# Where an attention step takes in another stream's transposes, and where their copy out of PSUM stands

## The chip, the cores and the metric

The kernel runs on one core of a Trainium2 chip. Its time is the device time of one execution in microseconds (us), the median of several. A core has engines with instruction queues of their own: TensorE (PE in the profile; PEld are its weight loads), VectorE (DVE), ScalarE (ACT), GpSimd (POOL) and SyncE (SP, which here only issues DMAs). TensorE writes to PSUM, from where ScalarE or VectorE have to copy a result before its PSUM buffer can be used again. An engine runs its instructions in the order of its queue, and an instruction that waits for another engine holds up all that are queued behind it.

## The reference

16 graphs of 1024 nodes with 128 features, and a dense 1024 x 1024 weighted adjacency matrix for each:

```python
h = relu(layernorm(x))
# layer 0: attention with 8 heads, masked and weighted by the adjacency
scores = where(adj == 0, -inf, q @ k.T / sqrt(16))        # each head
attn = softmax(scores) * adj
attn = attn / (attn.sum(-1) + 1e-8)
x = x + (attn @ v) @ Wo.T + bo
# layer 1: "dilation" of the adjacency, then three graph convolutions
h = relu(layernorm(x))
for n in range(1024):                                      # each graph, row after row
    num = row.sum();  sf = ceil(num / 2) if num > 10 else 1
    rm = row & (cumsum(row) % sf == 0) & (num > 1)         # edges of row n to remove
    carry[n] &= ~rm;  carry[:, n] &= ~rm                   # in the row and in the column
adj_d = adj * carry
for i in 1, 2, 3:
    h = batchnorm(relu(l2norm((adj_d @ h / deg) @ Wr + h @ Wx + b)))
x = x + concat(h1, h2, h3) @ Wl + bl
```

Attention and dilation both need the adjacency alone of the big inputs, and neither needs the other's result.

## The kernel before

The function `swept` does all of it, in two stages. In the first, which fills about the first 2330 us, two streams of work share the engines: `attention()` and `dilation()`, both generators. `beside_attention` (L951) runs them: after each step of the attention it lets the dilation go on to its next `yield`, for as long as the dilation's spent cost (the first number of each `yield`) is below its share. The second value of a `yield` says when the dilation may go on: 0 at once, 1 after the next attention step, "A" after the next step with even number, "B" after the next with odd number. For TensorE, ScalarE and VectorE the order in which the program issues instructions is the order of the queue (a "manual schedule"). The order on SP and POOL is set by a planner. The second stage, the graph convolutions, follows and isn't touched.

**The attention** goes through 16 graphs x 2 halves of the queries x 8 blocks of 128 keys, and for each through two groups of four heads, g = 0 and g = 1. So there are 512 steps; g = 0 are the even ones ("A") and g = 1 the odd ones ("B"). One step issues, in this order:

- `scores` (L539), on TensorE: 16 small matmuls put the mask into two PSUM tiles `sc` (L554), eight more add the score products (L560). There are two buffers of `sc`, just these two tiles, so the scores of a step can start only as the exponentials of the step before have read them: the first half of the mask matmuls needs the first exponential done, the second half the second.
- for g = 0, a normalization's two ScalarE instructions (L288), if one is due, and the transposes of an adjacency tile (`turn_over`, L505) on TensorE; for g = 1, a TensorE piece of the preparation of the next graph or of the conclusion of the last (`go_on_with(True)`: transposes or products, such as L401, L414, L333, L424).
- `values` (L484) of the step before, on TensorE: L487 and L492, which need that step's VectorE products `w` and exponentials `e`.
- two exponentials `e` (L598) on ScalarE, each over 128 x 1024 of `sc`, and then two products `w` (L603) on VectorE.
- the copies out of PSUM of the pieces above, on ScalarE (`go_on_with("evict")`); for g = 0 `aT` (L508) and `nomask` (L512) with their DMAs on SP, of which six shift the mask by partitions.

**The dilation** goes through eight blocks of 128 rows, for all 16 graphs together. In a block it first finds what each row removes within the block (VectorE mostly), and there it has transposes of its own: `pd` (L772) and `pr` (L878), two batches of eight bf16 transposes each in a block, into the PSUM tile `ps_d` of which there is one. Then it goes graph by graph through the 16 matrices, in a loop of 18 turns `i` (L896 to L949) that is a small pipeline. A turn has two parts. The first is issued after an A step: a scan of matrix i (`pair_sums`, L900, VectorE), and for matrix i - 2 eight transposes of its removal rows `er` (`pe`, L907, TensorE) and their copy `et` (L909, ScalarE, 128 x 1024 bf16). Then it yields "B". The second part is issued after the B step: two activations `wr` of matrix i (L915, ScalarE), the rows `er` of matrix i - 1 (L924 to L930, VectorE), the reading of the next block's adjacency rows as signs for matrix i - 2 (`read`, L699 and L703, ScalarE), the update of the diagonal of `er` with `et` (L937, VectorE), the stores of `er` and `et` to `mr_d` (L938 to L942, SP), `survive` (L716, VectorE), and loads for the next turns.

So in the kernel before, TensorE meets the transposes L907 between the values in an A step and the scores of the B step that follows; ScalarE meets the copy L909 after the A step's `nomask` and before the B step's exponentials.

Of the kernel before, what the change touches and what calls it, by code (L numbers as in the profile page):

```python
# [11 lines left out]
BF = mybir.dt.bfloat16  # L12
# [4 lines left out]
ALU = mybir.AluOpType  # L17
# [4 lines left out]
P = 128  # L22
# [12 lines left out]
def swept(ctx: ExitStack, tc: tile.TileContext, t: dict, out: bass.AP, flag: bass.AP):  # L35
# [8 lines left out]
    nc = tc.nc  # L44
    x, adj, nodemask = t["x"], t["adj"], t["nodemask"]
    B, N, D = x.shape
    H = 8
    HD = D // H
    NB = N // P
# [13 lines left out]
    ident_bf = const.tile([P, P], BF, name="ident_bf")  # L63
# [99 lines left out]
    ps_d = ctx.enter_context(tc.tile_pool(name="ps_d", bufs=1, space=PSUM))  # L163
# [3 lines left out]
    def first_part(p1):  # L167

        pool = p1.enter_context(tc.tile_pool(name="p1", bufs=2))
# [294 lines left out]

        beside = []

        def take_on(steps, at):
            beside.insert(at, [steps, next(steps)])

        def go_on_with(*kinds):  # L470


            for steps in beside[::-1] if kinds == ("first",) else beside:
                if steps[1] in kinds:
                    steps[1] = next(steps[0], None)
                    if steps[1] is None:
                        beside.remove(steps)
                    return

        def attention():  # L480
# [86 lines left out]
            for i, (b, c, m) in enumerate(turns):  # L567
                if m == 0:
                    if c == 0:
                        xt, _, _, v1 = ready[b]  # L570
                    acc = [ps_o.tile([P, HN], F32, name=f"acc_{b}_{c}_{g}", tag=f"acc{g}") for g in range(2)]
                    if c == 0 and b + 1 < B:
                        take_on(prepare(b + 1), len(beside))
                    if c == 1 and b + 1 == B:
                        take_on(begin_sage(), len(beside))
                if c == 1 and m == HB + 1:
                    load_x(b + 2)
                load(i + 3)
                aT = tiles[i][0]
                for g in range(2):  # L580
                    scs = scores(i, g)
                    go_on_with(f"half {c}")
                    if g == 0:
                        go_on_with("first")
                        turning = turn_over(i + 2)
                        next(turning, None)
                    else:
                        go_on_with(True)
                    if late:
                        values(*late)  # L590
                    elif g == 0:
                        go_on_with(True)
                    if (i, g) == (2, 0):
                        node_masks()
                    es, ws = [], []
                    for q in range(2):
                        e = pool.tile([P, 2, HN], F32, name=f"e_{b}_{c}_{m}_{g}_{q}", tag="e", bufs=4)
                        nc.scalar.activation(e, scs[q], AF.Exp, scale=1.0 / math.sqrt(HD))  # L598
                        es.append(e)
                    go_on_with("evict by VectorE")  # L600
                    for q in range(2):
                        w = pool.tile([P, 2, HN], F32, name=f"w_{b}_{c}_{m}_{g}_{q}", tag="w", bufs=4)
                        nc.vector.tensor_tensor(w, es[q], aT.to_broadcast([P, 2, HN]), ALU.mult)  # L603
                        ws.append(w)
                    late = (acc, v1, m, g, es, ws)
                    if m == 0 and g == 0 and i > 0:

                        take_on(conclude(*done), 1 if c == 0 else 0)
                        go_on_with(False)
                    go_on_with("evict")  # L610
                    if g == 0:
                        next(turning, None)
                    go_on_with(False)
                    if i + g + 1 < len(turns):
                        made["next"] = partial(scores, i + g, 1 - g)
                    yield
                tiles.pop(i)
                done = (b, c, acc, xt)
# [21 lines left out]
        def twice(ap):  # L640

            return ap.unsqueeze(2).to_broadcast([P, B, 2])
# [8 lines left out]
        def dilation():  # L651
# [84 lines left out]
            for k in range(NB):  # L736
# [3 lines left out]
                dgs = [rks[i][:, :, 2 + n0 : 2 + n1] for i in range(2)]  # L740
                halves = [slice(0, B // 2), slice(B // 2, B)]

                up = shared.tile([P, B, P], F16, name=f"up_{k}", tag="mr", bufs=4)
# [7 lines left out]
                next(late, None)  # L751
                yield 1.3, 1
                w = shared.tile([P, B, P], F16, name=f"w_{k}", tag="mr", bufs=4)
                pd = None
                for hb in halves:
                    nc.vector.tensor_tensor_scan(
                        w[:, hb, :].rearrange("p b i -> p (b i)"),
# [5 lines left out]
                    yield 2.3, 1  # L763
                for _ in late:
                    pass
                valid = shared.tile([P, B, P], BF, name=f"valid_{k}", tag="mr", bufs=4)
                cs = small.tile([P, 6, B], F32, name=f"cs_{k}", tag="cs", bufs=2)
                total, most, half, onw, last1, prev = (cs[:, i, :] for i in range(6))
                for c, hb in enumerate(halves):
                    pd = ps_d.tile([P, B // 2, P], BF, name=f"pd_{k}_{c}", tag="d")  # L770
                    for b in range(B // 2):
                        nc.tensor.transpose(pd[:, b, :], dgs[c][:, b, :], ident_bf)  # L772
                    if c == 0:
                        nc.vector.tensor_scalar(onw, w[:, :, P - 1], 1024.0, None, ALU.subtract)
                        for dg, of in zip(dgs, halves):
                            nc.vector.tensor_reduce(last1[:, of], dg, AX.X, ALU.add)
                    else:

                        nc.vector.tensor_tensor(total, left, right, ALU.add)
                        nc.vector.tensor_tensor(total, total, last1, ALU.add)  # L780
                        nc.vector.tensor_tensor(most, total, kill[:, :, k], ALU.add)
                        nc.vector.tensor_tensor(onw, onw, right, ALU.add)
                        nc.vector.scalar_tensor_tensor(half, total, -0.5, onw, ALU.mult, ALU.add)
                        nc.vector.tensor_scalar(half, half, 0.25, None, ALU.add)
                        end16 = small.tile([P, B, 2], F16, name=f"end16_{k}", tag="at16", bufs=2)
                        nc.vector.tensor_scalar(end16, twice(onw), 1024.0, None, ALU.add)
                    yield (2.5 if c == 0 else 1.4), 1
                    nc.vector.tensor_tensor(valid[:, hb, :], pd, up[:, hb, :], ALU.mult)
                    yield 0.7, 1 - c

                nc.vector.tensor_tensor(valid, valid, each(beyond), ALU.mult)
# [7 lines left out]
                hit = shared.tile([P, B, P], BF, name=f"hit_{k}", tag="mr", bufs=4)  # L799
# [6 lines left out]
                for r in range(ROUNDS):  # L806
# [3 lines left out]
                    num, y, c, high, lost = (v[:, i, :] for i in range(5))  # L810
# [62 lines left out]
                nc.vector.tensor_tensor(hit, hit, valid, ALU.add)  # L873
                yield 2.5, 1
                for c, hb in enumerate(halves):
                    pd = ps_d.tile([P, B // 2, P], BF, name=f"pr_{k}_{c}", tag="d")
                    for b in range(B // 2):
                        nc.tensor.transpose(pd[:, b, :], hit[:, c * B // 2 + b, :], ident_bf)  # L878
                    yield 0.0, 1
                    nc.vector.tensor_tensor(dgs[c], dgs[c], pd, ALU.subtract)  # L880
                    yield 0.7, (1 if c == 0 else "A")


# [3 lines left out]
                wrs, gms, ers, ets = {}, {}, {}, {}  # L887

                def known(b):

                    if k > 0 and b < B:
                        gms[b] = shared.tile([P, N], BF, name=f"gm_{k}_{b}", tag="gm", bufs=2)
                        nc.sync.dma_start(gms[b][:, :n0], mr_d[b][:, k, :n0])

                known(0)
                for i in range(B + 2):  # L896
                    b = i
# [4 lines left out]
                        )  # L902
                    b = i - 2
                    if 0 <= b:
                        pe = ps_d.tile([P, NB, P], BF, name=f"pe_{k}_{b}", tag="d")
                        for j in range(NB):
                            nc.tensor.transpose(pe[:, j, :], ers[b][:, j * P : (j + 1) * P], ident_bf)  # L907
                        ets[b] = pool.tile([P, NB, P], BF, name=f"et_{k}_{b}", tag="et", bufs=2)
                        nc.scalar.copy(ets[b], pe)  # L909
                    yield (1.3 if i < B else 0.0), "B"  # L910
                    b = i
                    if b < B:
                        wrs[b] = pool.tile([P, N], F16, name=f"wr_{k}_{b}", tag="wr", bufs=2)
# [5 lines left out]
                    b = i - 1  # L919
# [12 lines left out]
                    b = i - 2  # L932
                    if 0 <= b:
                        if more:
                            read(k + 1, b)
                        er, et = ers.pop(b), ets.pop(b)
# [275 lines left out]
    with tc.manual_schedule(  # L1212
# [178 lines left out]
        for b in range(B):  # L1391
            pys = products(b)
            of = [pys[k // HB][:, (k % HB) * P : (k % HB + 1) * P] for k in range(NB)]
# [584 lines left out]
```

## Time and profile before

| | us |
|---|---|
| median of 3 runs | 3399.15 (3396.95 to 3402.11) |
| the profiled execution | 3396.91 |
| its span, from first to last instruction | 3395.1 |
| busy in the span: PE, DVE, ACT | 3310.6, 3025.5, 2305.4 |
| granted TensorE clock, share of full | 0.995 |
| copies `et` (L909), 128 of them | 127.2 busy, the first starts at 190.4, the last at 2285.2 |
| transposes `pe` (L907), 1024 of them | 79.4 busy, 18.2 idle before them |
| exponentials (L598), 1024 of them | 991.9 busy, 333.6 idle before them |

A line of the waits names the engine and the line that waited, then after `<-` the one that released it, and the total in us, how often and the longest. A line of the timeline has the start in us, the duration, the engine and line, the operation, `out<-in`, the shapes of out and in, and how many instructions in a row it merges; `[0.22 <-ACT e L598]` is the idle time of that engine just before, and what ended it. Neighbours on ScalarE overlap by some 0.1 us in these records, so a start can lie before the end of the line above. Matmuls are pipelined, and a busy TensorE isn't one at its peak.

### The profile page before, as it was taken

The page shows a single profiled execution, that of the slowest core. Times are in us where ns is not written, and L with a number is a line of the kernel's source. Part 1 is how long each engine was busy: PE and PEld are TensorE (multiplying, and loading weights), DVE is VectorE, ACT ScalarE, POOL GpSimd, SP SyncE. Part 2 cuts the span into 40 slices and gives each one's busy share as a digit, 9 for nine tenths or more (in the row PEclk, how much of TensorE's full clock was granted, in tenths as well). Part 3 has the DMA queues.
Part 4 walks back from the last instruction along what each step waited for, and adds up shares of the span by engine and source line. Part 5 has one row for each costly group of instructions (what it writes and reads, how often), then busy time and mean ns, then how long its engine had stood idle before and what let it go on. Part 6 is the DMA issues. An engine that isn't in the chain of part 4 may idle for free. (4 is left out here: it accounts for less than half of the span.)

```text
span 3395.1 us, 86338 instructions
## 1 busy us (share of the span) xinstructions
PE 3310.6 (98%) x34855; PEld 1872.4 (55%) x34855; DVE 3025.5 (89%) x5399; ACT 2305.4 (68%) x3909; POOL 164.2 (5%) x253
## 2 busy tenths in 40 slices
PE   8999999999999999999999999999999899999997
PEld 3333333333333333333334334336999899999997
DVE  7898989989989998998998999897888899988887
ACT  7699689779879969968976986884232344423334
POOL 2000000000000000000000000000000000000000
PEclk9999999999999999999999999999999999999999
DMA  7357456547637736845863773677999799989996
GB/s 242 108 168 206 137 149 199 161 129 221 188 122 213 221 122 183 238 144 158 236 190 122 237 240 119 189 228 261 346 341 343 284 353 350 353 323 350 352 351 222
DMA packets 650123, 772.28 MB, mean 227 GB/s; under 512 B 173264, under 2 KB 569168, under 8 KB 637424
## 3 DMA queue, kind: packets, MB, share of 16 engines
q1 hardware_dynamic: 632672, 708.58, 64.4%
q0 software_dynamic: 15456, 57.30, 5.0%
q8 instruction: 275, 4.51, 0.6%
q14 instruction: 136, 1.11, 0.1%
q10 hardware_dynamic: 1584, 0.79, 0.1%
HBM read 508.50 MB, written 157.29 MB: 196 GB/s over the span
## 5 line engine op out<-in xcount | busy, mean ns | idle before, releaser
L603 DVE TENSOR_TENSOR w<-e,aT 128x1024 f32<-128x1024 f32 x1024 | 1205.5, 1219 | 138.4 <-ACT e L598 136.8
L598 ACT ACTIVATE e<-sc 128x1024 f32<-128x1024 f32 x1024 | 991.9, 1022 | 333.6 <-PE sc L560 332.6
L1132 PE MATMUL pg<-y,aT 128*128 128x128 f32 (+1 forms) x6144 | 729.8, 275 | 0.0
L1132 PEld LDWEIGHTS pg<-y,aT 128*128 128x128 f32 x6144 | 707.9, 192 | 0.0
L487 PE MATMUL acc<-w,both 128*32 128x512 f32 x4096 | 586.7, 605 | 3.1 <-DVE w L603 2.6
L560 PE MATMUL sc<-qT,kT 32*128 32x512 f32 x4096 | 584.4, 640 | 0.3 <-ACT qT L315 0.3
L492 PE MATMUL acc<-e,eps 128*32 128x512 f32 x4096 | 573.1, 592 | 0.0
L146 DVE SCALAR_TENSOR_TENSOR aT<-mr,aT 128x1024 f32<-128x1024 bf16 x384 | 458.8, 1217 | 0.0
L492 PEld LDWEIGHTS acc<-e,eps 128*32 128x32 f32 x4096 | 150.6, 110 | 294.6 <-issue 289.6
L1155 ACT ACTIVATE sq<-o 128x512 f32<-128x512 f32 x96 | 60.6, 631 | 328.5 <-DVE o L1150 328.5
L554 PEld LDWEIGHTS <-never 32*32 32x32 bf16 x8192 | 80.9, 88 | 347.9 <-issue 325.6
L554 PE MATMUL sc<-nomask,never 32*32 32x512 bf16 x8192 | 252.3, 385 | 16.8 <-ACT e L598 12.3
L1173 ACT COPY hT<-pt 128x512 f32<-128x512 f32 x96 | 56.3, 586 | 289.3 <-PE pt L1169 280.0
L560 PEld LDWEIGHTS sc<-qT,kT 32*128 32x128 f32 x4096 | 160.1, 183 | 116.9 <-issue 116.1
L505 PEld LDWEIGHTS pa<-ident,a 128*128 128x128 f32 x1024 | 107.7, 141 | 181.4 <-issue 129.7
L487 PEld LDWEIGHTS acc<-w,both 128*32 128x32 f32 x4096 | 92.8, 108 | 156.2 <-issue 65.4
L915 ACT ACTIVATE wr<-both,th 128x512 f16<-128x512 f16 x256 | 172.1, 730 | 7.1 <-DVE both L900 6.9
L505 PE MATMUL pa<-ident,a 128*128 128x128 f32 x1024 | 168.3, 287 | 6.4 <-DMA a<-in_adj 5.7
L512 ACT ACTIVATE nomask<-aT 128x512 bf16<-128x512 f32 x256 | 161.4, 630 | 8.1
L1150 DVE SCALAR_TENSOR_TENSOR o<-pg,rdeg,mine 128x128 f32<-128x128 f32 x384 | 108.1, 344 | 55.9 <-PE pg L1132 52.6
L508 ACT COPY aT<-pa 128x512 f32<-128x512 f32 x256 | 152.7, 597 | 5.3 <-PE pa L505 4.3
L900 DVE TENSOR_TENSOR_SCAN both<-rk 128x513 f16<-128x513 bf16 x128 | 155.9, 1218 | 0.0
(228 smaller groups left out, 3894.9 us busy)
## 6 DMA issues: line engine op xcount, KB each, us to landing
aT<-aT_d SPq DMA_DIRECT2D x94, 2048.0 KB, 9.9
mr<-mr_d SPq DMA_DIRECT2D x188, 512.0 KB, 6.0
aT_d<-aT SPq DMA_DIRECT2D x256, 256.0 KB, 4.0
a<-in_adj SPq DMA_DIRECT2D x253, 256.0 KB, 3.7
ad<-in_adj SPq DMA_DIRECT2D x112, 512.0 KB, 4.2
nomask<-nomask SPq DMA_DIRECT2D x512, 96.0 KB, 2.7
nomask<-nomask SPq DMA_DIRECT2D x512, 64.0 KB, 2.7
nomask<-nomask SPq DMA_DIRECT2D x512, 32.0 KB, 2.7
```

The costliest lines, as they stand in the source:

```text
L146: nc.vector.scalar_tensor_tensor(part, mrs[h][:, j : j + 2, :].rearrange("p j n -> p (j n)"), 0.0, part, ALU.is_equal, ALU.mult)
L487: nc.tensor.matmul(acc[g][32 * j : 32 * j + 32, :], v1[:, m, (2 * j + g) * HW : (2 * j + g) * HW + 32], ws[j // 2][:, j % 2, :], start=(m ...
L492: nc.tensor.matmul(acc[g][32 * j : 32 * j + 32, :], eps8, es[j // 2][:, j % 2, :], start=False, stop=(m == NB - 1),)
L505: nc.tensor.transpose(pa[:, k * P : (k + 1) * P], a[:, k, :], ident)
L512: nc.scalar.activation(nomask[:, 0, :], aT[:, 0, :], AF.Relu, bias=1.0, scale=-1e38, accum_out=zeros[:, i : i + 1])
L554: nc.tensor.matmul(scs[j // 2][to : to + 32, j % 2, :], never[rows, rows], nomask[rows, j, :], start=True, stop=False, tile_position=(32 * ...
L560: nc.tensor.matmul(scs[j // 2][:, j % 2, :], kT[rows, mm], qTs[c][rows, g, :], start=False, stop=True, tile_position=(32 * j, 0),)
L598: nc.scalar.activation(e, scs[q], AF.Exp, scale=1.0 / math.sqrt(HD))
L603: nc.vector.tensor_tensor(w, es[q], aT.to_broadcast([P, 2, HN]), ALU.mult)
L900: nc.vector.tensor_tensor_scan(pair_sums[b % 2], row[:, 0::2], row[:, 1::2], 0.0, ALU.add, ALU.add)
L915: nc.scalar.activation(wrs[b][:, t * HN : (t + 1) * HN], pair_sums[b % 2][:, t : t + HN], AF.Abs, bias=at[:, b : b + 1], scale=2.0,)
L1132: nc.tensor.matmul(pg[:, i // 2, at : at + width], aT[:, j, i * P : (i + 1) * P], y[:, j, :width], start=(j == 0), stop=(j == NB - 1),)
```

## The change

Two lists of work are added beside the attention: `ahead_of_values` and `behind_exponentials`. The dilation no longer issues its transposes itself but puts them on the first list, and the copy `et` on the second. The attention's next step issues the first list just ahead of `values`, after the scores and the step's own transposes, and the second behind its exponentials, products and other copies. Where the dilation goes on before that, it issues what is left itself. For matrix i - 2 this means: the transposes L907 move on TensorE from ahead of the scores of the B step to behind them, ahead of the values; the copy moves on ScalarE from ahead of the B step's exponentials to behind them, ahead of the second part's `wr`. The transposes `pd` and `pr` move in the same way by part of a step; VectorE still reads them from PSUM itself.

```diff
+        ahead_of_values, behind_exponentials = [], []
+
+        def run(work):
+            while work:
+                work.pop(0)()
...
+                    run(ahead_of_values)
                     if late:
                         values(*late)
...
                     go_on_with("evict")
                     if g == 0:
                         next(turning, None)
+                    run(behind_exponentials)
                     go_on_with(False)
...
+                pds = []
+
+                def across(name, c):
+                    pd = ps_d.tile([P, B // 2, P], BF, name=f"{name}_{k}_{c}", tag="d")
+                    for b in range(B // 2):
+                        of = dgs[c][:, b, :] if name == "pd" else hit[:, c * B // 2 + b, :]
+                        nc.tensor.transpose(pd[:, b, :], of, ident_bf)
+                    pds.append(pd)
...
-                    pd = ps_d.tile([P, B // 2, P], BF, name=f"pd_{k}_{c}", tag="d")
-                    for b in range(B // 2):
-                        nc.tensor.transpose(pd[:, b, :], dgs[c][:, b, :], ident_bf)
+                    ahead_of_values.append(partial(across, "pd", c))
...
-                    nc.vector.tensor_tensor(valid[:, hb, :], pd, up[:, hb, :], ALU.mult)
+                    run(ahead_of_values)
+                    nc.vector.tensor_tensor(valid[:, hb, :], pds.pop(), up[:, hb, :], ALU.mult)
...
-                    pd = ps_d.tile([P, B // 2, P], BF, name=f"pr_{k}_{c}", tag="d")
-                    for b in range(B // 2):
-                        nc.tensor.transpose(pd[:, b, :], hit[:, c * B // 2 + b, :], ident_bf)
+                    ahead_of_values.append(partial(across, "pr", c))
                     yield 0.0, 1
-                    nc.vector.tensor_tensor(dgs[c], dgs[c], pd, ALU.subtract)
+                    run(ahead_of_values)
+                    nc.vector.tensor_tensor(dgs[c], dgs[c], pds.pop(), ALU.subtract)
...
+                def transposed(b):
+                    pes[b] = ps_d.tile([P, NB, P], BF, name=f"pe_{k}_{b}", tag="d")
+                    for j in range(NB):
+                        nc.tensor.transpose(pes[b][:, j, :], ers[b][:, j * P : (j + 1) * P], ident_bf)
+
+                def emptied(b):
+                    ets[b] = pool.tile([P, NB, P], BF, name=f"et_{k}_{b}", tag="et", bufs=2)
+                    nc.scalar.copy(ets[b], pes.pop(b))
...
-                        pe = ps_d.tile([P, NB, P], BF, name=f"pe_{k}_{b}", tag="d")
-                        for j in range(NB):
-                            nc.tensor.transpose(pe[:, j, :], ers[b][:, j * P : (j + 1) * P], ident_bf)
-                        ets[b] = pool.tile([P, NB, P], BF, name=f"et_{k}_{b}", tag="et", bufs=2)
-                        nc.scalar.copy(ets[b], pe)
+                        ahead_of_values.append(partial(transposed, b))
+                        behind_exponentials.append(partial(emptied, b))
                     yield (1.3 if i < B else 0.0), "B"
+                    run(ahead_of_values)
+                    run(behind_exponentials)
```

More of the change, by code (lines that the diff above doesn't have):

```diff
@@ L753, in dilation @@
                 w = shared.tile([P, B, P], F16, name=f"w_{k}", tag="mr", bufs=4)
-                pd = None
                 for hb in halves:
@@ L893, in known @@
                         nc.sync.dma_start(gms[b][:, :n0], mr_d[b][:, k, :n0])
+                pes = {}
+                def transposed(b):
[5 more added lines that the diff above has]
+                    nc.scalar.copy(ets[b], pes.pop(b))
                 known(0)
```

## The prediction

> **What bounds the kernel now.** I read the page's busy shares first, then the chain of waits, then the busy time by stretch of the span, and last the timeline of one stretch, engine by engine.
>
> ```profile
> PE 3310.6 (98%) x34855; PEld 1872.4 (55%) x34855; DVE 3025.5 (89%) x5399; ACT 2305.4 (68%) x3909; POOL 164.2 (5%) x253
> ```
>
> Over the whole span TensorE looks like the only bound. The waits seem to say the same, and to promise a gain:
>
> ```profile
> ACT e L598 <- PE sc L560: 332.6, 284, 4.0
> ...
> PE pe L907 <- DVE er L930: 18.0, 35, 1.2
> PE sc L554 <- ACT e L598: 12.3, 33, 0.5
> ```
>
> The moved transposes (L907) wait 18.0 us in all for their rows on VectorE, the scores (L554) 12.3 us for exponentials; ScalarE idles 332.6 us for scores. But these are sums over stages. The copies of `et` (L909) show where the moved work runs: eight blocks of some 138 us, 16 copies each, with some 140 us between them without any. The table by stretch has those two kinds in turn (columns: stretch, length, then busy us of PE, PEld, DVE, ACT, POOL with their counts, clock, DMA share, GB/s):
>
> ```profile
> 190.00:328.00 138.00, 135.10 (x1481) 49.86 (x1478) 123.85 (x204) 136.81 (x241) 4.78 (x5) 1.00 0.68 196
> 328.00:465.00 137.00, 136.50 (x1620) 50.44 (x1612) 122.19 (x213) 99.71 (x152) 7.01 (x8) 1.00 0.43 132
> ...
> 1866.00:2011.00 145.00, 139.49 (x1484) 52.24 (x1481) 141.00 (x221) 136.78 (x212) 4.97 (x6) 1.00 0.80 241
> ...
> 2152.00:2286.00 134.00, 131.09 (x1465) 47.56 (x1464) 127.50 (x178) 118.73 (x173) 8.28 (x13) 1.00 0.74 222
> ```
>
> Where the copies run, ScalarE is busy 136.81 of 138 us: it is the bound there, and its idle time lies in the stretches between (99.71 of 137), which have TensorE as the bound and no copies. In the later blocks VectorE joins (141.00 of 145); in the last, ScalarE has slack (118.73 of 134). So the question is what the change does to ScalarE's 9 us per matrix in the blocks. One such period, ScalarE alone:
>
> ```profile
> 1103.62 1.93 ACT L598 ACTIVATE e<-sc 128x1024 f32<-128x1024 f32 x2
> 1105.43 0.60 ACT L508 COPY aT<-pa 128x512 f32<-128x512 f32 x1
> 1106.06 0.63 ACT L512 ACTIVATE nomask<-aT 128x512 bf16<-128x512 f32 x1
> ...
> 1106.69 0.99 ACT L909 COPY et<-pe 128x1024 bf16<-128x1024 bf16 x1
> 1107.59 1.94 ACT L598 ACTIVATE e<-sc 128x1024 f32<-128x1024 f32 x2
> 1109.40 1.34 ACT L915 ACTIVATE wr<-both,th 128x512 f16<-128x512 f16 x2
> ...
> 1111.86 0.88 ACT L288 ACTIVATE xt<-xt,rs_b 128x128 f32<-128x128 f32 x2
> 1112.63 1.92 ACT L598 ACTIVATE e<-sc 128x1024 f32<-128x1024 f32 x2
> ```
>
> No gap anywhere: exponentials of the first head group (g = 0, end 1105.55), aT, nomask, et, exponentials of g = 1 (end 1109.53), then wr, the signs, a normalization, and the next g = 0 (end 1114.55). The period is 9.00 us. TensorE answers like this:
>
> ```profile
> 1105.61 0.41 PE L554 MATMUL sc<-nomask,never 32*32 32x512 bf16 x8 [0.22 <-ACT e L598]
> 1105.94 1.14 PE L560 MATMUL sc<-qT,kT 32*128 32x512 f32 x8
> ```
>
> The second half of the next scores can start only when the last exponential has left its PSUM buffer: 0.06 us after 1105.55. Score products follow at 1105.94, and elsewhere exponentials that find ScalarE idle start 1.17 or 1.18 us after that (1182.66 to 1183.83, 1196.99 to 1198.16). So from the end of one pair of exponentials to the start of the next no less than 0.06 + 0.33 + 1.17 = 1.56 us can pass. The trace has a gap without a copy in it that shows this floor:
>
> ```profile
> 2141.07 1.94 ACT L598 ACTIVATE e<-sc 128x1024 f32<-128x1024 f32 x2
> ...
> 2143.51 0.63 ACT L512 ACTIVATE nomask<-aT 128x512 bf16<-128x512 f32 x1
> ...
> 2144.57 1.94 ACT L598 ACTIVATE e<-sc 128x1024 f32<-128x1024 f32 x2 [0.33 <-PE sc L560]
> ```
>
> End 2143.01, next start 2144.57: 1.56 us, only aT and nomask in it, ScalarE idle at its end. Of all 511 gaps between pairs none is shorter.
>
> **The change, part by part.** No instruction is added or removed. TensorE's L907, pd and pr transposes move, ScalarE's 128 copies move, VectorE's and POOL's order stays; on SP some loads and stores change places with neighbours.
>
> *The copy.* It now stands behind the exponentials of g = 1, not ahead of them. Ahead of them it took 1107.59 - 1106.69 = 0.90 us of the gap g = 0 to g = 1, which lasted 1107.59 - 1105.55 = 2.04 us. Without it ScalarE has aT and nomask to do, done 1106.69 - 1105.55 = 1.14 us after the exponentials; but the scores arrive at 1.56. The gap shrinks by 2.04 - 1.56 = 0.48 us and not by 0.90; ScalarE stands idle 0.42 us. In the gap g = 1 to g = 0, 1112.63 - 1109.53 = 3.10 us and full, the copy adds 0.90. Net 0.90 - 0.48 = +0.42 us a matrix. The copy was the work that hid the turnaround of the scores; the other gap, already twice the floor, needs no cover.
>
> TensorE doesn't stop this. From scores g = 1 (1105.61) its work is 1.40 for the scores, 0.59 for one 4-tile transpose, 0.55 for L907 and 1.85 for the values: next scores at 4.4 us, exponentials possible 1.5 later, at some 6.0. ScalarE comes to them only at 1.56 + 1.94 + 4.00 = 7.5. TensorE just waits longer.
>
> How many pay? By the gaps of ScalarE's timeline, of 80 matrices in blocks 0 to 4, 47 have both gaps full (mean 2.03 first gap): 47 x 0.42 = 19.7 us. In 14 the first gap already has idle time (mean 2.37) and the second is full: without the 0.55 to 0.62 of L907 ahead of the scores it falls to between 1.56 and 1.82, net +0.1 to +0.35, taken as 0.2: 2.8. Ten have two oT copies in the first gap (aT, nomask and these last 2.1, above the floor): nothing. In nine the second gap has some 0.4 us to spare already: nothing. Blocks 5 and 6: ten full (4.2) and five mixed (1.0). Block 7: three, 0.6. Sum 28.3.
>
> *The transposes of L907.* They no longer hold up the scores for a late row. Of their 18.0 us of waiting some 12.4 lies in blocks 5 to 7 (4.5, 5.5 and 2.4 by the timeline). In block 7 TensorE is the bound and 2.4 comes back. In blocks 5 and 6 VectorE is 97% busy, and its order is unchanged; its idle time, 4.6 + 4.0, caps the gain. From 0 to -8.6, I take -2, near the low end, as ScalarE there is as full. In blocks 0 to 4 the wait is behind ScalarE and worth nothing.
>
> Here the Trainium skill speaks the other way. Perfetto Trace Analysis, section Optimization Strategy, says: find the gaps on the engine you are optimizing, see what each waits for, and make that come sooner. Read on the page's 98% TensorE, that rule gives all of 18.0 + 12.3 = 30.3 us: 3369. The same section warns that the most contended engine can change between regimes; the table by stretch shows it does, and then the rule is to be applied to ScalarE, whose gaps the change opens. I go by the table: +24.
>
> *pd and pr.* 32 batches of eight, 0.55 us each, in stretches where TensorE is the bound: same work, one place later. Cover: pd was ready at 1182.36 and used at 1190.30 (L788); one step later it is ready near 1185. pr was made at 155.9 and used at 161.3; it keeps over 2 us. Value 0; if the cover went, at most 32 x 0.6 = 19 us.
>
> *What queues behind the copy.* The wr pair (0.90 later against the exponentials, 0.42 against the period), the signs, the normalization, exponentials: that is the sum above. The VectorE row update L937 uses `et` at 1113.1; the copy now ends about 4.3 after 1105.55, at 1109.9: 3 us of cover. SP's two stores of `et` went out at 1111.12, behind the mask moves that hold SP until 1111.02; 1109.9 is still ahead. If that cover went, SP's loads of `ad` and `gm` behind them would be late, by less than a copy (0.9) a matrix. The other SP swaps are by a few places among issues of 0.3 to 0.6 us, with rows read two periods (18 us) after their load: 0.
>
> *Sum.* 28.3 - 2.4 - 2 = +23.9. The profiled execution took 3396.91 us (span 3395.1), so 3420.8; it lies 2.2 under the median of 3399.15, to which the same +24 gives **3423**. With the bounds: 19.7 alone less 11 gives +9; 28.3 with five more for copies that wait on a long TensorE piece, +33.
>
> **The rivals.** *TensorE's waits are what counts (faster).* L907's 18.0 us comes back and no floor is paid: 3399 - 18 = 3381, with the scores' 12.3 too, 3369. For it: 98% on the page. Against: ScalarE full in the blocks. It decides if the second gap has more than 0.42 us to spare on average; that is so in block 7 only (1.0).
> *Nothing moves (3399).* ScalarE idles over a quarter of the stretches between the blocks, and losses of 0.42 could be taken up. Against: 1.2 us idle in the 138 of block 0.
> *VectorE is starved as well (slower still).* wr was ready at 1110.74 with VectorE coming to it at 1111.03. After the change wr is 0.42 later, 0.13 too late here, and 0.3 to 0.8 too late where VectorE has no normalization beside it. ScalarE's lengthening hides that, unless VectorE is the bound (blocks 3 to 6, 64 matrices): 64 x 0.4 = 26 on top, 3449.
>
> **How the numbers follow.** Copy's cover lost, +9 to +33: 0.63 (3408 to 3432, likeliest 3423). Faster: 0.13. No change: 0.12. VectorE too: 0.12. A measurement tells 0.2% (7 us) from no change; of the main case 0.02 falls inside. Slower 0.73, same 0.14, faster 0.13. The range leaves out most of the faster case and the far end of the starved one: 3390 to 3446.
>
> **What would show it.** Right: in the blocks the gap g = 0 to g = 1 near 1.56 with ScalarE idle 0.4 before exponentials, the other gap near 4.0, the period 9.0 going to 9.4, blocks 0 to 4 each some 4 to 5 us longer, the stretches between unchanged, L907's waits gone, TensorE's waits for exponentials up by tens of us. Wrong: first gaps filled by something that I don't see, periods of 9.0, or blocks shorter than before.

## The result, and the profile after

| us | before | after |
|---|---|---|
| median | 3397.51 (6 runs) | 3422.14 (6 runs, 3418.55 to 3426.26) |
| the profiled execution | 3396.91 | 3420.13 |
| its span | 3395.1 | 3418.3 |
| ratio of the times, 95% interval | | 1.0070 (1.0057 to 1.0083) |

The kernel became 24.6 us slower, 23.2 by the spans of the two profiled executions. The forecast was 3423. Line numbers of the changed kernel are 6 to 24 higher than before: exponentials L605, products `w` L610, mask matmuls L560, score products L566, transposes `pe` L914, copy `et` L918, signs L707 and L711, `survive` L724.

The busy line of the kernel after:

```profile
PE 3302.0 (97%) x34855; PEld 1878.7 (55%) x34855; DVE 3027.9 (89%) x5399; ACT 2309.1 (68%) x3909; POOL 163.9 (5%) x253
```

Counts are the same to the instruction and busy times within 9 us. No engine has more to do; the 23 us are waiting. The chain of waits says who waits:

```profile
ACT e L605 <- PE sc L566: 359.0, 346, 4.7
PE sc L560 <- ACT e L605: 61.7, 135, 0.8
...
DVE rk L724 <- DMA gl<-mr_d: 9.1, 4, 4.4
```

No line names the transposes `pe` any more: the 18.0 us that L907 waited for its rows are gone. In their place TensorE's wait for exponentials rose from 12.3 to 61.7 us, and ScalarE's wait for scores from 332.6 to 359.0. The two wait for each other more often. The third line is new in its size: VectorE waited 2.3 us for `gl` before.

Busy time by stretch of after (stretch, length, then PE, PEld, DVE, ACT, POOL with counts, clock, DMA share, GB/s), the stretches that answer to the four of before:

```profile
191.00:334.00 143.00, 134.09 (x1464) 50.06 (x1456) 123.73 (x205) 137.96 (x240) 4.77 (x5) 1.00 0.66 195
334.00:471.00 137.00, 136.50 (x1628) 51.80 (x1628) 121.89 (x211) 99.23 (x153) 6.81 (x7) 1.00 0.41 126
...
1891.00:2037.00 146.00, 141.83 (x1484) 52.54 (x1482) 142.25 (x224) 137.21 (x213) 4.96 (x6) 1.00 0.80 237
...
2182.00:2314.00 132.00, 130.99 (x1462) 49.88 (x1454) 126.86 (x177) 118.22 (x172) 8.25 (x13) 1.00 0.75 229
```

Block 0 now lasts 143 us where it lasted 138, and ScalarE has worked about as long in it: 1.2 us of idle time have become 5. The stretch behind it has kept its 137 us. Block 6 (third line) grew by 1 us, block 7 (last) lost 2. The granted clock is 1.00 in all of them, so it is not the clock.

The matrix that the prediction showed, on ScalarE of the kernel after:

```profile
1116.51 1.92 ACT L605 ACTIVATE e<-sc 128x1024 f32<-128x1024 f32 x2
1118.32 0.59 ACT L514 COPY aT<-pa 128x512 f32<-128x512 f32 x1
1118.94 0.63 ACT L518 ACTIVATE nomask<-aT 128x512 bf16<-128x512 f32 x1
...
1120.00 1.94 ACT L605 ACTIVATE e<-sc 128x1024 f32<-128x1024 f32 x2 [0.34 <-PE sc L566]
1121.82 1.02 ACT L918 COPY et<-pe 128x1024 bf16<-128x1024 bf16 x1
1122.71 1.35 ACT L939 ACTIVATE wr<-both,th 128x512 f16<-128x512 f16 x2
...
1125.18 0.87 ACT L288 ACTIVATE xt<-xt,rs_b 128x128 f32<-128x128 f32 x2
1125.95 1.92 ACT L605 ACTIVATE e<-sc 128x1024 f32<-128x1024 f32 x2
```

From the end of the exponentials of g = 0 (1118.43) to the start of those of g = 1 pass 1.57 us, with 0.34 of idle time that the scores end. The other gap, 1121.94 to 1125.95, is 4.01 and full. The period is 1125.95 - 1116.51 = 9.44 us; it was 9.00. TensorE in the same gap:

```profile
1118.49 0.41 PE L560 MATMUL sc<-nomask,never 32*32 32x512 bf16 x8 [0.51 <-ACT e L605]
1118.83 1.14 PE L566 MATMUL sc<-qT,kT 32*128 32x512 f32 x8
...
1120.39 0.61 PE L914 MATMUL pe<-ident_bf,er 128*128 128x128 bf16 x8
1120.93 1.06 PE L493 MATMUL acc<-w,both 128*32 128x512 f32 x8
```

TensorE stands ready for 0.51 us, gets the PSUM half 0.06 after the exponentials, and takes 0.34 for the mask; 1.17 after its first score product ScalarE goes on. That is the turnaround of 1.56 us, now without anything to hide it.

Over the whole trace: of 112 gaps g = 0 to g = 1 (the 16 with two more copies, of `oT`, left out) none was under 1.6 us before; after, 86 lie at 1.56, and the idle time in sum went from 14.7 to 46.2 us. The blocks of the two traces, each from its first scan to the first scan behind it:

| | blocks 0 to 4 | 5 and 6 | 7 | stretches ahead of 0 to 4 | ahead of 5, 6, 7 | the rest |
|---|---|---|---|---|---|---|
| growth, us | 5.7, 3.9, 5.0, 3.9, 3.7 | 1.4, 0.5 | -2.3 | -1.9, -0.2, -1.3, -0.3, -0.5 | 1.0, 1.7, 4.5 | -1.7 |
| sum | 22.2 | 1.9 | -2.3 | -4.2 | 7.2 | -1.7 |

The runs of the kernel after differ by up to 8 us, so differences of 1 or 2 us in one stretch mean nothing; the 22.2 of blocks 0 to 4 are the result.

The same two traces can be compared matrix by matrix, by the period from the start of a matrix's g = 0 exponentials to the next start of g = 0. In blocks 0 to 4 the 47 matrices that had both gaps full before grew by 0.44 us each, 20.7 in sum. The 14 that had idle time in the first gap alone grew by 4.3, the ten with two more copies of `oT` shrank by 0.9, and the nine with time to spare in the second gap shrank by 1.9. The sum is the 22.2 again.

### The profile page after: what moved, and what is told of

The parts are those of the page before. It is cut to its first block, busy times and chain, and to the rows that moved or that the text cites. A ratio compares the mean times of both kernels' runs of the same rounds, so it can differ in the third digit from the quotient of the medians.

```text
span 3418.3 us, 86347 instructions
## 1 busy us (share of the span) xinstructions
PE 3302.0 (97%) x34855; PEld 1878.7 (55%) x34855; DVE 3027.9 (89%) x5399; ACT 2309.1 (68%) x3909; POOL 163.9 (5%) x253
## 5 line engine op out<-in xcount | busy, mean ns | idle before, releaser
L610 DVE TENSOR_TENSOR w<-e,aT 128x1024 f32<-128x1024 f32 x1024 | 1205.6, 1219 | 155.6 <-ACT e L605 154.0
L605 ACT ACTIVATE e<-sc 128x1024 f32<-128x1024 f32 x1024 | 991.7, 1022 | 359.8 <-PE sc L566 359.0
L566 PE MATMUL sc<-qT,kT 32*128 32x512 f32 x4096 | 583.9, 640 | 0.5 <-ACT qT L315 0.5
L560 PEld LDWEIGHTS <-never 32*32 32x32 bf16 x8192 | 86.2, 87 | 523.9 <-issue 521.5
L560 PE MATMUL sc<-nomask,never 32*32 32x512 bf16 x8192 | 265.3, 384 | 64.3 <-ACT e L605 61.7
L566 PEld LDWEIGHTS sc<-qT,kT 32*128 32x128 f32 x4096 | 159.9, 182 | 116.9 <-issue 116.1
```

The costliest lines, as they stand in the source:

```text
L560: nc.tensor.matmul(scs[j // 2][to : to + 32, j % 2, :], never[rows, rows], nomask[rows, j, :], start=True, stop=False, tile_position=(32 * ...
L566: nc.tensor.matmul(scs[j // 2][:, j % 2, :], kT[rows, mm], qTs[c][rows, g, :], start=False, stop=True, tile_position=(32 * j, 0),)
```

## The experiments

The theory: the copy in the gap g = 0 to g = 1 was cover for the scores' turnaround, on a ScalarE that has no time to spare in a block. The main rival: the values come later behind the transposes, and what follows from them is late. All times are medians; each ratio is against the kernel before, run on the same chip beside it.

**The copy alone.** The kernel before, with the copy behind the exponentials; all transposes stay where they were.

```diff
                     go_on_with("evict")
                     if g == 0:
                         next(turning, None)
+                    run(behind_exponentials)
...
-                        nc.scalar.copy(ets[b], pe)
+                        behind_exponentials.append(partial(emptied, b))
```

> Only the copy et moves behind the exponentials of g = 1; all transposes stay where they were before the change. Lost cover (the copy hid the turnaround of the scores on ScalarE): the gap g = 0 to g = 1 falls to 1.56 us as with the whole change, so the loss is there too, and the transposes' waits for late rows aren't won back: 3420 to 3430 us, 23 to 32 above the kernel before. Late values (the rival: what costs is that the eight transposes now stand ahead of the values on TensorE): no loss, 3390 to 3404 us.

Measured: 3430.62 against 3397.26, ratio 1.0093 (1.0076 to 1.011). The values are not behind the transposes here, and the whole loss is there, with 8.7 us on top (33.4 against 24.6). So late values fall as the cause. The waits of this kernel:

```profile
PE sc L560 <- ACT e L604: 41.0, 96, 0.7
PE pe L920 <- DVE er L944: 13.0, 26, 1.1
```

The transposes wait 13.0 us for their rows again, and 74 of the 112 gaps are at 1.56 us where the change has 86: with the transposes ahead of them the scores sometimes come later than the floor, and the idle time in these gaps is 63.3 us where the change has 46.2. So moving the transposes is a gain once the copy has moved, of about 9 us by the medians (from 1 to 16 by the two intervals), and moving the copy is the loss.

**`pd` and `pr` alone.** The changed kernel with `pe` and `et` issued in their old places.

```diff
-                        ahead_of_values.append(partial(transposed, b))
-                        behind_exponentials.append(partial(emptied, b))
+                        transposed(b)
+                        emptied(b)
```

> Only the transposes pd and pr (32 batches of eight) are taken in by the next attention step; L907 and its copy stay as before the change. The prediction puts this at 0: within 4 us of the kernel before. If moved transposes cost time by standing ahead of the values, at most 32 x 0.6 = 19 us.

Measured: 3396.61 against 3399.38, ratio 0.9995 (0.9986 to 1.0003): nothing, as the prediction had it.

**More work for ScalarE, in the open gap and in the full one.** Two small copies (128 x 88, their result used by nobody) in each of the 128 gaps, in the kernel after and in the kernel before. If ScalarE idles for the turnaround, they are free in the first and paid in the second.

```diff
+        pad = one.tile([P, 88], BF, name="pad")
...
+                        for _ in range(2):
+                            nc.scalar.copy(pad, attn_w[:, 0, :88])
                     yield (1.3 if i < B else 0.0), "B"
```

In the kernel after:

> The whole change, with two extra ScalarE copies (128 x 88, together some 0.33 us, their result used by nobody) in each of the 128 gaps g = 0 to g = 1 from which the copy was taken. Lost cover: ScalarE stands idle 0.36 us in that gap anyway, so the extra work is free: within 3 us of the whole change's 3422. If it is just the sum of ScalarE's work that counts: 128 x 0.33 = 42 us at most, some 25 to 35 above it, 3447 to 3457.

Measured: 3433.06, ratio 1.0107 (1.009 to 1.0124), 10.9 over the changed kernel and not 3 at most. In the kernel before:

> The kernel before, with the same two extra ScalarE copies in the same 128 gaps, behind et. Lost cover: this gap is full in the kernel before (2.04 us of work and none idle), so the extra work is paid where ScalarE is the bound, 0.33 us in 60 to 90 of 128 matrices: 20 to 30 us, 3417 to 3427. So the kernels before and after should end up within some 5 us of each other with the filling in both. If the filling were hidden here too: 3398.

Measured: 3423.09, ratio 1.0072 (1.0055 to 1.0089), 25.8 over the kernel before. Timeline of ScalarE, fill in the kernel before:

```profile
1123.55 0.99 ACT L910 COPY et<-pe 128x1024 bf16<-128x1024 bf16 x1
1124.45 0.56 ACT L912 CAST pad<-attn_w 128x88 bf16<-128x88 f32 x2
1124.91 1.93 ACT L599 ACTIVATE e<-sc 128x1024 f32<-128x1024 f32 x2
```

And fill in the kernel after:

```profile
1124.81 0.54 ACT L934 CAST pad<-attn_w 128x88 bf16<-128x88 f32 x2
1125.26 1.93 ACT L606 ACTIVATE e<-sc 128x1024 f32<-128x1024 f32 x2
```

The pair takes 1124.91 - 1124.45 = 0.46 us of ScalarE, not the 0.33 it was made for. In the kernel before the full gap went from 2.03 to 2.50 us. By the periods of the traces the 56 matrices with both gaps full (the prediction counted 60) paid 0.46 us each, 25.6 in sum; the 16 with the `oT` copies paid 5.5, and the rest, which had idle time in a gap, gave 4 back. In the kernel after the pair is a little larger than the idle time: the gap went from 1.56 to 1.59. The same 56 matrices paid 0.04 us each there, 2.1 in sum, and the 16 with the `oT` copies, which leave no idle time in their gap in either kernel, paid 6.8. The miss is the size of the fill and the 16 gaps that the expectation left out; in the open gaps the fills were nearly free, and in the kernel before they were not.

**Other work as cover.** The changed kernel, with the signs of the next block (two activations, L707 and L711, 1.2 us) moved from the second part of a turn into the opened gap.

```diff
                         behind_exponentials.append(partial(emptied, b))
+                        if more:
+                            read(k + 1, b)
                     yield (1.3 if i < B else 0.0), "B"
...
-                        if more:
-                            read(k + 1, b)
```

> The whole change, and the reading of the next block's rows as signs (two ScalarE activations a matrix, 1.23 us) taken from behind the copy to the gap that the copy left, ahead of the exponentials of g = 1. Lost cover: the gap has 1.14 + 1.23 = 2.37 us of work, over the floor of 1.56, ScalarE is full again, the other gap is 3.10 + 0.90 - 1.23 = 2.77 us, the period 9.0: the loss goes, and some of the transposes' 12 us of waits in blocks 5 to 7 is won: 3385 to 3399 us. Late values: the transposes still stand ahead of the values, so the loss stays, 3415 to 3425 us.

Measured: 3585.44, ratio 1.0547 (1.0529 to 1.0564): 188 us slower than before, a miss by far. The waits of this kernel, and SP's own:

```profile
PE sc L560 <- DMA nomask<-nomask: 86.6, 122, 3.7
...
SPq L718 <- DMA mr_d<-et: 303.3, 112, 4.9
```

SP's wait in the changed kernel for the same thing:

```profile
SPq L718 <- DMA mr_d<-et: 55.3, 58, 3.1
```

L718 is the load of `gl`, which must not start before the stores of `et` to `mr_d` have landed. All 112 of these loads now wait, 2.7 us each. The timeline of SP shows what stands behind:

```profile
1205.47 0.65 SPq L907 DMA_DIRECT2D gm<-mr_d  x1
1206.22 0.45 SPq L962 DMA_DIRECT2D mr_d<-er  x1
1209.26 0.32 SPq L718 DMA_DIRECT2D gl<-mr_d  x1
...
1210.15 0.45 SPq L515 DMA_DIRECT2D aT_d<-aT  x1
1210.70 0.53 SPq L522 DMA_DIRECT2D nomask<-nomask  x1
```

SP is held from 1206.67 to 1209.26 by `gl`, and the adjacency tile and the mask moves of the attention queue up behind it; the mask matmuls of all heads wait for them. The load of `ad` (L691) now goes out at 1203.84, ahead of the two stores of `et` (1204.47 and 1204.90), where it stood behind them in the changed kernel. So activations that were moved by half a turn changed SP's order, and the load that waits for a landing blocks the ones that nobody delays. The granted clock of this run was 0.977, against 0.995 before; what part of the 188 us the clock has is not separated.

**The same with `gl` on another queue.** As above, but the loads of `gl` are issued by GpSimd, which has little else to do.

```diff
-                    nc.sync.dma_start(gl[:, : k * P], mr_d[b][:, k, : k * P])
+                    nc.gpsimd.dma_start(gl[:, : k * P], mr_d[b][:, k, : k * P])
```

> The kernel of the signs in the gap once more, with the loads gl (the rows that wait for a store of et to land) issued on POOL's queue instead of SP's. There SP stood at gl with the mask moves behind it, since a load of ad went out ahead of the stores of et. If that, and not the signs or the transposes, made it slow, the 188 us go: lost cover gives 3385 to 3399 us, the kernel before or better. Late values: 3415 to 3425. If the signs in the gap themselves cost: over 3500.

Measured: 3399.99 against 3399.38, ratio 1.0002 (0.9994 to 1.001). The 188 us are gone, and the 24 of the change as well. It is 1 us above the range expected, 3385 to 3399: the loss is undone, but nothing of the transposes' waits shows as a gain. ScalarE's wait for scores is back near the 332.6 us of before:

```profile
ACT e L605 <- PE sc L566: 330.7, 270, 9.4
```

Timeline of ScalarE in this kernel:

```profile
1101.93 0.59 ACT L514 COPY aT<-pa 128x512 f32<-128x512 f32 x1
1102.55 0.63 ACT L518 ACTIVATE nomask<-aT 128x512 bf16<-128x512 f32 x1
...
1103.18 0.72 ACT L707 ACTIVATE rk<-ad 128x640 bf16<-128x640 f32 x1
...
1103.90 0.51 ACT L711 ACTIVATE rk<-ad 128x384 bf16<-128x384 f32 x1
...
1104.41 1.92 ACT L605 ACTIVATE e<-sc 128x1024 f32<-128x1024 f32 x2
1106.21 1.01 ACT L918 COPY et<-pe 128x1024 bf16<-128x1024 bf16 x1
```

The gap is full again, with the signs in the copy's place, and the copy still stands behind the exponentials. TensorE's order is that of the change:

```profile
1102.43 1.14 PE L566 MATMUL sc<-qT,kT 32*128 32x512 f32 x8
...
1104.00 0.61 PE L914 MATMUL pe<-ident_bf,er 128*128 128x128 bf16 x8
1104.54 1.07 PE L493 MATMUL acc<-w,both 128*32 128x512 f32 x8
```

So neither the place of the transposes nor that of the copy costs anything that these runs can tell, as long as the turnaround is covered. That holds if `gl` on GpSimd alone does nothing, which the next two say.

**`gl` on GpSimd alone.** The same one line, in the kernel before and in the kernel after. In the kernel before:

> The kernel before, with only the loads gl on POOL's queue: what that queue alone does. Nothing in the kernel before waits for gl on SP for long (VectorE 2.3 us in all): within 4 us of the kernel before, so that the signs in the gap and VectorE's copies are to be read against the kernel before as they stand. If POOL's queue delays its normalizations or the loads: 3 to 10 us slower.

Measured: 3398.8 against 3398.15, ratio 1.0001 (0.9992 to 1.0009). In the kernel after:

> The whole change, with only the loads gl on POOL's queue instead of SP's. In the change VectorE waits up to 4.4 us at the start of the last block for a gl that stands on SP behind a late store of et and the mask moves; the stretches between the later blocks grew by 1.0, 1.7 and 4.5 us. If SP's order is the cause, these 5 to 7 us go and the loss in the blocks stays: 3412 to 3419. If not: 3422.

Measured: 3423.18, ratio 1.0064 (1.0051 to 1.0078): no change against 3422.14, where 3412 to 3419 was expected if SP's order makes `gl` late. The signs kernel differs from this one by the place of the signs alone, so the 23 us between them (3423.18 to 3399.99) come from the signs. In the changed kernel VectorE waits for `gl` as a block ends (timeline of VectorE, after):

```profile
2046.50 2.28 DVE L763 TENSOR_TENSOR_SCAN w<-go_on,up 128x1024 f16<-128x1024 bf16 x1
2053.18 1.09 DVE L724 SCALAR_TENSOR_TENSOR rk<-rk,gl 128x896 bf16<-128x896 bf16 x1 [4.39 <-DMA gl<-mr_d]
```

With `gl` on GpSimd that one waits 1.92 us:

```profile
2057.43 1.09 DVE L724 SCALAR_TENSOR_TENSOR rk<-rk,gl 128x896 bf16<-128x896 bf16 x1 [1.92 <-DMA gl<-mr_d]
```

But VectorE's waits for `gl` in sum did not fall:

```profile
DVE rk L724 <- DMA gl<-mr_d: 11.8, 5, 4.3
```

The stretches ahead of blocks 5, 6 and 7 came out at 2.9, 3.7 and 2.9 us over before, 9.5 in sum against 7.2. So the queue that issues `gl` isn't the whole of what makes it late there. Both kernels load `gl` behind the same landing of `et`; what part of that is the copy's place is worked out below.

**The copy off ScalarE.** If ScalarE alone is the bound in a block, taking the copy away from it must win. In blocks 0 to 2 VectorE copies `et`, just before it uses it; blocks 3 to 7 are as before.

```diff
+                        if k < 3:
+                            ets[b] = pool.tile([P, NB, P], BF, name=f"et_{k}_{b}", tag="et", bufs=2)
+                            nc.vector.tensor_copy(ets[b], pes.pop(b))
                         er, et = ers.pop(b), ets.pop(b)
```

> In blocks 0 to 2 the transposes are ahead of the values as in the change, and VectorE copies et out of PSUM (some 0.7 us) in the turn's second part, so ScalarE has no copy; in blocks 3 to 7 transposes and copy stand as before the change. If ScalarE is the bound of the early blocks, its period falls from 9.0 to 9.0 - 0.90 + 0.42 (the gap at its floor) = 8.5, VectorE comes to 8.0 + 0.7 = 8.7: 0.3 us x 45 = some 14 us under the kernel before, 3380 to 3390. If TensorE is the bound there: 3397.

Measured: 3447.73, ratio 1.014 (1.0125 to 1.0155), slower by 48 where 14 less were expected. Its waits show the trouble of the signs kernel in small:

```profile
PE sc L560 <- DMA nomask<-nomask: 21.9, 37, 2.1
...
SPq L718 <- DMA mr_d<-et: 123.0, 68, 4.2
```

So the same with `gl` on GpSimd:

> The kernel with VectorE's copies in blocks 0 to 2 once more, with the loads gl on POOL's queue. There the stores of et came after the masks' turn, the gl behind them waited on SP and the mask moves were late (TensorE waited 21.9 us for masks). If that made it slow and ScalarE is the bound of blocks 0 to 2: 10 to 15 us under the kernel before, 3384 to 3390. If TensorE or VectorE bounds these blocks as well: 3397 to 3402. If VectorE's copy itself costs: about 3447 again.

Measured: 3398.22 against 3398.15, ratio 1.0002 (0.9994 to 1.001). The stall is gone, and there is no gain either. Busy by stretch of this kernel, block 0:

```profile
190.00:328.00 138.00, 136.25 (x1503) 51.49 (x1501) 135.44 (x226) 127.77 (x232) 13.74 (x21) 1.00 0.71 204
```

ScalarE has 10 us to spare in 138, and the block is as long as before, with TensorE at 136.3 and VectorE at 135.4. By the cut from scan to scan, blocks 0 to 2 changed by -2.8, -1.2 and 2.8 us. Relieving ScalarE in a block is worth nothing by this route. Which of the other two engines holds the block is not separated: TensorE was at 135.1 before, and the copies took VectorE from 123.9 to 135.4. None of these kernels is faster than the kernel before.

## Why the prediction was right

Its likeliest case was 3423, at 3422.14 measured, and most parts of the sum agree as well:

| part | predicted | measured |
|---|---|---|
| blocks 0 to 4, cover lost (19.7 + 2.8) | 22.5 | 22.2 |
| blocks 5 and 6 (4.2 + 1.0 - 2) | 3.2 | 1.9 |
| block 7 (0.6 - 2.4) | -1.8 | -2.3 |
| `pd` and `pr`, alone (a run of its own, not in the sum) | 0 | -2.8, no change by its interval |
| between and around the blocks | 0 | 1.3 (of it 7.2 ahead of blocks 5 to 7) |
| sum | 23.9 | 23.1 |

The closeness of the first row is in part luck. The matrices with both gaps full lost 20.7 us where 19.7 was forecast, and the 14 mixed ones 4.3 where 2.8 was; the others, forecast at nothing, gave 2.8 back.

*The reading of the bound* held for what the change does: work or idle time added to ScalarE in a full block is paid. As "the bound" it said too much. In the prediction's own line for block 0 TensorE has 135.10 us of 138 beside ScalarE's 136.81, and with ScalarE relieved to 127.77 the block stayed as long. TensorE's 98% and its 30 us of waits promised 3369; L907's 18.0 us of waiting for rows did go away, and TensorE waits 49.4 us more for exponentials instead. The rule in the Trainium skill, Perfetto Trace Analysis, section Optimization Strategy, to go for the gaps of the engine that is to be made faster, works here only with the engine that the stretch names, as the section's own words "within the timestamps of the regime of interest" ask.

*The floor* of 1.56 us is where 86 of 112 gaps now lie. The idle time was forecast at 0.42 us a matrix and the line shows 0.34: ScalarE reads out nomask's accumulator for another 0.1 us, which the forecast left out, though its own line of the gap without a copy shows 0.33. The growth of the period doesn't depend on this; it was forecast at 0.42 and is 0.44.

*That the idle time is what costs*, and nothing else late, was shown from both sides: work put into it is nearly free after and paid before, and other work in it takes the loss away.

*The transposes' own gain* was put at 4.4 us in blocks 5 to 7. Undone alone it measures 8.7. By the traces 6.7 of that lie in the 22 matrices, of all blocks, whose first gap alone had idle time before; the prediction has these in another term, as scores that come sooner. So the 4.4 were not measured by themselves.

*The step that failed* is the one that gave the copy's later end no price on SP ("1109.9 is still ahead", "0"). It was argued from one matrix in the middle of a block, and the stretches between the blocks were forecast unchanged. At the end of block 6 VectorE waits 4.39 us for the block's last `gl`, until 2053.18 (shown above), where the same instruction didn't wait before:

```profile
2026.05 1.07 DVE L716 SCALAR_TENSOR_TENSOR rk<-rk,gl 128x896 bf16<-128x896 bf16 x1
```

The stretch ahead of block 7 grew by 4.5 us. It goes with the place of the copy: the same stretch grew by 5.1 us with the copy moved alone and by 4.2 with the fill in the kernel after, and by 0.0 in the three kernels that leave the copy in place (the fill in the kernel before, `pd` and `pr` alone, `gl` on GpSimd in the kernel before). The block's last copy and the issue of that `gl`, before:

```profile
2010.12 0.99 ACT L909 COPY et<-pe 128x1024 bf16<-128x1024 bf16 x1
...
2021.99 0.32 SPq L710 DMA_DIRECT2D gl<-mr_d  x1
```

And after:

```profile
2035.76 1.02 ACT L918 COPY et<-pe 128x1024 bf16<-128x1024 bf16 x1
...
2049.72 0.32 SPq L718 DMA_DIRECT2D gl<-mr_d  x1
```

Counted from the end of the copy, VectorE came to this `gl` after 2026.05 - 2011.11 = 14.9 us, and now is ready for it after 2048.78 - 2036.78 = 12.0. The copy has moved 2.9 us towards its use. The load went out 10.9 us after the copy and now goes out after 12.9; why these 2 us came on top stays open. The stretches ahead of blocks 5 to 7 grew by 7.2 us together, and those ahead of the other blocks and the rest shrank by 5.9, so the total hides the error.

*The rivals.* "TensorE's waits are what counts" and "nothing moves" fell with the result. "VectorE is starved as well" would have put 26 us on blocks 3 to 6; they grew by 9.5 in all, about what the cover alone gives.

## What to carry to other kernels

A copy that stands between two dependent steps of other engines may be what hides their turnaround: before moving it, work out how short the gap can get without it (here 1.56 us), and what else would fill it. Where two engines are both near full in a stretch, as TensorE and ScalarE here, taking work off one can be worth nothing, while idle time put on it was paid in full by the matrices that had none to spare. So look at the busy time stretch by stretch, not over the span. And before moving work that has transfers, look at which load on the same queue waits for a store to land, for all that is issued behind it waits too.

## What the hardware did that was not expected

- Two activations moved half a turn earlier cost 188 us through SP's order: 112 loads that waited 2.7 us each for a store's landing, with the masks behind them (303.3 us of SP's waits against 55.3). One changed queue for these loads took all of it back.
- VectorE copies the 128 x 1024 bf16 tile out of PSUM in 0.68 us, ScalarE in 0.99. It didn't matter for the time.
- Two ScalarE copies of 128 x 88 out of SBUF take 0.46 us of its queue, half of what one 128 x 1024 copy out of PSUM takes (0.90), for a sixth of its elements.
- A load that itself waits for a store's landing was not on the whole earlier when an idle queue issued it: with `gl` on GpSimd VectorE's waits for it were 11.8 us, with `gl` on SP 9.1, though the last of them fell from 4.39 to 1.92.
